# A quantile search over 32-bit masks: the bits and the count of a group in two sums over a constant in place of three sums

## The chip, the cores and the metric

The kernel runs on one NeuronCore of a Trainium2 chip. The metric is the device time of one execution in microseconds (us). Engines are named as in the profile: PE (matrix products) with PEld (its weight loads), DVE (vector), ACT (scalar, element by element), POOL and SP (here they mostly start DMA transfers). Sums of matrix products are made in PSUM, in banks of 512 float32 numbers per partition; ACT or DVE reads them out ("evicts" them).

## The reference

Four graph layers with a residual and a normalisation each, over 16 graphs of 1024 nodes with 64 channels. The change touches the third alone. There, every node takes, channel by channel, the 0.25, 0.5 and 0.75 quantiles of its neighbours' values (after some edges are dropped):

```python
vals = jnp.where(nd[..., None], x[:, None, :, :], jnp.inf)
s = jnp.sort(vals, axis=2)
nv = nd.sum(2)
agg = jnp.zeros_like(x)
for tau, w in zip(TAUS, WTS):
    pos = jnp.asarray(tau, x.dtype) * jnp.maximum(nv - 1, 0).astype(x.dtype)
    lo = jnp.floor(pos).astype(jnp.int32)
    hi = jnp.ceil(pos).astype(jnp.int32)
    ...
    agg = agg + jnp.asarray(w, x.dtype) * (v_lo + frac * (v_hi - v_lo))
```

`nd` is the neighbourhood matrix of a graph (1024 x 1024, zeros and ones), `lo` and `hi` are the places of the two values wanted among a node's sorted neighbours.

## The kernel before

Graphs go in pairs, eight pairs. For each pair the layers before the quantiles run first (attention takes most of their time), and beside the attention of one pair all 1024 node values of each channel of the pair ahead are sorted on DVE. Then the quantile stage of that pair runs (`quantiles`). This happens eight times.

*What the stage does.* For a channel, a node's neighbours are a set of ranks from 0 to 1023. The ranks are cut into 32 blocks (`T`) of 32 ranks (`R`). For each block and each node the kernel makes, by a matrix product with the neighbourhood matrix, a 32-bit mask (which ranks of this block are neighbours) together with a count (how many neighbours lie in earlier blocks). From the counts it finds the block in which the wanted neighbour lies, picks this block's mask, and searches the mask for the k-th set bit.

*Groups, pairs, units, steps.* Four channels make a group (`G` = 16 groups in a graph). A group with one of the three quantiles is a step; eight steps (`U8N`) make a unit. A stage has 96 steps, s = 0 to 7 in each of 12 units, and a group serves three steps, so a unit uses 8/3 groups.

*Elements and words.* `words_of` (L1086), at the end of the sort, splits a rank into block `rk` and place `r16` within the block, and makes from the place the powers of two that stand for its bit, by writing exponents of bfloat16 numbers as integers. `words` (L771) makes the weights `E` of a group on DVE, 128 x 1024 elements in one tile for each piece of the mask. The first is 16 for a rank in an earlier block, a power of two for the ranks 0 to 3 of the block itself, and 0 for later blocks (L786 and L787: a difference, clamped to 0 and 16). The second and third hold the ranks 4 to 17 and 18 to 31 (L789 and L791: a comparison, and a product with `b_w` for each). Up to seven such tiles (`EB`) are alive.

`half_word` (L854) sums one piece over all nodes, for half of the 1024 columns: eight matmuls with the neighbourhood matrix `ndT` into one bank, then one eviction (L862) that adds 8192 and writes uint16, so that, read as bfloat16, the piece is an ordinary number that a product with 0 or 1 leaves as it is. A group has three pieces, two halves each: six half sums of at most 14 bits.

*A step, s, on PE.* The order of PE's products in the loop is written out (`product`): `distances` for the step twelve back (`r,pen`, `kilo,pen`, `oh,bd`, four banks), the first part of the step's half sums, `least_values`, `one_hot` of the next step (`lt,dif`, four banks), `sum_values` (`vals,bonesf`), the rest of the half sums, and `sum_words` (`wps<-m,tonesb`). All banks come from one pool of four, in turn. `MORE` says how many half sums a step gets: (4, 3, 3, 3, 1, 1, 1, 0).

*A step on DVE.* `compare` (L867) finds by `lt` which blocks begin at or before the wanted place; `dif` on PE makes the difference of neighbouring blocks, ACT copies it as `oh` (one 1 per column); `pick` (L885) multiplies all three pieces by `oh`, once for each of the two places, into `m`; `sum_words` adds over the blocks. `lt` has one buffer, `m` has two, one for each of the two places.

*The bit search.* When a unit's eight steps are summed, ACT copies the sums (`wb`, L710) and `kth_bit` (L700) runs on DVE, in parts over the steps 0 to 4 of the next unit. It subtracts the 8192, takes the count from the first piece, and finds the k-th bit by counting bits in parts. Its last operations write `r64` and `r2` (L768, L769), which `distances` reads from step 4 on (`r,pen`). `more_elements` is called in the steps 4 to 7, but the order on DVE is set when the kernel is built, by priorities, and not by the place of the call.

Of the kernel before, what the change touches and what calls it, by code (L numbers as in the profile page):

```python
# [14 lines left out]
F16 = mybir.dt.float16  # L15
BF = mybir.dt.bfloat16
I32 = mybir.dt.int32
U16 = mybir.dt.uint16
# [12 lines left out]
T = 32  # L31
R = 32
NW = 3
OFF = 8192.0
G = C // 4
NQ = 3
U8N = 8
# [1 line left out]
GB = 4  # L39
PARTS = 4  # L40
LAG = PARTS + 1
MORE = (4, 3, 3, 3, 1, 1, 1, 0)
SC = 2048.0
VB = 4
EB = 7
# [15 lines left out]
def shape_constants():  # L61

    bf = ml_dtypes.bfloat16
    s = np.arange(N)
    t = np.arange(T)
    x = np.arange(8 * P)[None, :] - 3 * P
    tc = np.broadcast_to(t[:, None], (T, 2))

    p = np.arange(P)
    dif = np.eye(P) - ((p[:, None] == p[None, :] + 2) & (p[:, None] // C == p[None, :] // C))  # L70

    tones = np.zeros((P, U8N, 32))
# [12 lines left out]


    tof = np.zeros((2, 2, U8N, 4, NU, C))
    qrow = np.zeros((2, 2, U8N, 4, 3, 4))
    for u in range(NU):
        for i in range(U8N):  # L90
            g, q = divmod(U8N * u + i, NQ)
            for c in range(4):
                tof[:, :, i, c, u, 4 * g + c] = 1.0
            share = 0.25 * (q + 1)
            w = (0.25, 0.5, 0.25)[q] / SC
            for kk in range(2):
                qrow[:, kk, i, :, u % 3, :] = (share, kk - share - 0.375, -w, w)
    return {
        "c_t": np.broadcast_to(tc, (P, T, 2)).astype(np.uint16),
        "c_t16": np.broadcast_to(16.0 * tc, (P, T, 2)).astype(np.float16),  # L100
        "c_dif": dif.astype(bf),
        "c_bones": bones.astype(np.float32),
        "c_tones": tones.astype(bf),
        "c_tones4": tones[:, 0, :4].astype(np.float16),
        "c_pen": pen.reshape(P, U8N, 3, P).astype(np.float16),
        "c_tof": tof.reshape(P, NU, C).astype(np.float32),
        "c_qrow": qrow.reshape(P, 3, 4).astype(np.float32),
        "c_place": (np.sign(x - p[:, None]) + 1.0).astype(bf),
        "c_id": np.eye(P, dtype=np.float32),
        "c_idb": np.eye(P, dtype=np.float32).astype(bf),  # L110
        "c_idh": np.eye(P, dtype=np.float16),
        "c_iota": np.broadcast_to(s.astype(np.float16), (P, N)).copy(),
    }
# [3 lines left out]
def gnn_kernel(ctx: ExitStack, tc: tile.TileContext, a: dict, out: bass.AP):  # L117
# [22 lines left out]
    t16_c = load("t16_c", [P, T, 2], F16, a["c_t16"])  # L140
# [29 lines left out]
    tones4 = load("tones4", [P, 4], F16, a["c_tones4"])  # L170
    kilo = const.tile([P, 1], F16, name="kilo")
    nc.vector.memset(kilo, 1024.0)
    bn_a = const.tile([P, C], F32, name="bn_a")
    bn_b = const.tile([P, C], F32, name="bn_b")

# [42 lines left out]
    def bank(shape, dtype=F32):  # L218
        return ps1.tile(shape, dtype, name="bank")
# [439 lines left out]
    def rank_limits(gr, qe, qn):  # L659
# [14 lines left out]
        def limits(q):  # L674

            lim = gr.lim[q] = qe.tile([P, 2, N], U16, name="lim", bufs=LB)
            nc.scalar.activation(lim[:, 0], cnt, AF.Copy, scale=0.25 * (q + 1), bias=-0.25 * (q + 1) - 0.375)
            for s in (1, 0):
                nc.vector.tensor_scalar(lim[:, s], lim[:, 0], 16.0, OFF + 16.0 * (s + 1), op0=ALU.mult, op1=ALU.add)

        def weights(t):
            if t == 0:
# [17 lines left out]
    def kth_bit(pool, wps, kd, r2, r64):  # L700
# [9 lines left out]
        nc.scalar.copy(wb, wps)  # L710
        yield
        X = wb.bitcast(U16)
        v.tensor_scalar(X, X, OFF, None, op0=ALU.subtract)
        k = u16("k")
        S = u16("S", [P, 2, 512])
        U = u16("U", [P, 2, 512])
        a, c = U[:, 0], S[:, 0]
        v.tensor_scalar(a, X[:, 0], 4, None, op0=ALU.logical_shift_right)
        v.tensor_tensor(k, kd, a, ALU.subtract)
        v.tensor_scalar(X[:, 0], X[:, 0], 15, None, op0=ALU.bitwise_and)  # L720

        def counts(x, s1, s2, s4, t):

# [25 lines left out]
        v.tensor_scalar(pos, M[:, 0], 4.0, None, op0=ALU.mult)  # L749
# [21 lines left out]
    def words(pool, g, ws, rk, u_w, b_w):  # L771


        sh = [P, 2 * NB, T, 2]
        E = [pool.tile([P, NB, P], BF, name="E", bufs=EB) for w in ws]
        Ev = [e.rearrange("p j (h t c) -> p (j h) t c", h=2, t=T) for e in E]

        def over_t(x):
            return x[:, g].rearrange("p j (h c) -> p (j h) c", h=2)[:, :, None, :].to_broadcast(sh)

        def over_j(x):
            return x[:, None].to_broadcast(sh)

        if ws == [0]:
            d = Ev[0].bitcast(F16)
            nc.vector.tensor_tensor(d, over_j(t16_c), over_t(u_w), ALU.subtract)  # L786
            nc.vector.tensor_scalar(Ev[0], d, 0.0, 16.0, op0=ALU.max, op1=ALU.min)  # L787
        else:
            nc.vector.tensor_tensor(Ev[1], over_t(rk), over_j(t_c), ALU.is_equal)  # L789
            for w in range(2):  # L790
                nc.vector.tensor_tensor(Ev[w], Ev[1], over_t(b_w[w]), ALU.mult)  # L791
        return E

    def quantiles(ip, rk, u_w, b_w):
# [12 lines left out]
        with ExitStack() as es:  # L807
# [46 lines left out]
            def half_word(gr, g, w, hf, matmul):  # L854

                if (w, hf) == (0, 0):
                    gr.V[g] = qe.tile([P, NW, N], U16, name="V", bufs=VB)
                cols = slice(hf * 512, (hf + 1) * 512)
                ps = bank([P, 512])
                for j in range(NB):  # L860
                    matmul(ps, gr.E[g][w][:, j], gr.ndT[:, j, cols], start=(j == 0), stop=(j == NB - 1))
                nc.scalar.activation(gr.V[g][:, w, cols], ps, AF.Copy, bias=OFF)  # L862

            def compare(u, s):
                gr, g, q = u.pairs[s]
# [79 lines left out]
            halves = iter([(k, w, hf) for k in range(len(groups)) for w in range(NW) for hf in range(2)])  # L945
            todo = [(k, ws) for k in range(len(groups)) for ws in ([0], [1, 2])]
            made = used = 0

            def elements():

                nonlocal made
                k, ws = todo.pop(0)
                gr, g = groups[k]
                gr.E.setdefault(g, []).extend(words(qe, gr.bb * G + g, ws, rk, u_w, b_w))
                made += len(ws)

            def more_elements():
                while todo and made + len(todo[0][1]) <= used // 2 + EB:
                    elements()

            def more_words(n, matmul=product):
# [6 lines left out]

            load_matrix(graphs[0])
            with tc.high_priority():  # L970
                while made < 2 * NW:
                    elements()
            more_words(2 * NW, nc.tensor.matmul)
            more_elements()
            counts, limits, weights = rank_limits(graphs[0], qe, qn)
            for hf in range(2):
# [11 lines left out]
            for i, (u, s) in enumerate(steps):  # L988
# [97 lines left out]
    def words_of(pool, rank, rk, u_w, b_w):  # L1086
# [9 lines left out]
        m = pool.tile([P, 2 * G, NB, 4], U16, name="m16")  # L1096
        e = pool.tile([P, 2 * G, NB, 4], U16, name="e16")
        z = pool.tile([P, 2 * G, NB, 4], U16, name="z16")
        for w, first in ((2, 18), (1, 4), (0, 0)):
            dst = z if w == 0 else b_w[w - 1].bitcast(U16)  # L1100
            if w < 2:
                v.tensor_scalar(m, r16, float((4, 18)[w]), None, op0=ALU.is_lt)
            if w == 2:
                v.tensor_scalar(e, r16, 18.0, None, op0=ALU.is_ge)
            elif w == 1:
                v.tensor_scalar(e, r16, 4.0, None, op0=ALU.is_ge)
                v.tensor_tensor(e, e, m, ALU.mult)
            else:
                e = m
            v.tensor_scalar(dst, r16, float(127 - first), 128.0, op0=ALU.add, op1=ALU.mult)  # L1110
            v.tensor_tensor(dst, dst, e, ALU.mult)
        v.tensor_scalar(u_w, rk, 16.0, None, op0=ALU.mult)
        v.tensor_tensor(u_w, u_w, z.bitcast(BF), ALU.subtract)

    def sort(keys, pool, key, pace, rk, u_w, b_w):
# [52 lines left out]
        return key  # L1168

    rk = keep.tile([P, 2 * G, NB, 4], U16, name="rk")  # L1170
    u_w = keep.tile([P, 2 * G, NB, 4], F16, name="u_w")
    b_w = [keep.tile([P, 2 * G, NB, 4], BF, name=f"b_w{w}") for w in range(2)]

    def sort_keys(srt, ip):
        key = srt.tile([P, N], F32, name="key", bufs=2)
# [103 lines left out]
```

## Time and profile before

| | us |
|---|---|
| runs of before, median of 3 | 13250.63 (13241.73 to 13259.92) |
| the profiled execution | 13256.31 |
| its span | 13254.3 |
| PE busy in the span | 11579.9 (87%) |
| DVE busy | 10669.6 (80%) |
| ACT busy | 7184.3 (54%) |
| one quantile stage, 2835 to 3804 us: length | 969.0 |
| PE, DVE, ACT busy in it | 872.9, 831.7, 541.8 |

In a line of a group the profile shows the source line, the engine, the operation, what is written and read, the shape, how often it occurs, busy time and the mean duration of one (ns), and then how long the engine was idle just before and what ended that. In a timeline a row begins with the start and the busy time of a run of equal instructions; a wait ahead of it stands in brackets. Mean durations overlap: the next instruction starts before the last has ended, so the distance between starts is what one more costs.

### The profile page before, as it was taken

Reading aid. Unit: us, or ns where it says so; the run is one execution under the profiler, and the core shown is the slowest. Engines: PE = TensorE matmul, PEld = TensorE weight load, DVE = VectorE, ACT = ScalarE, POOL = GpSimd, SP = SyncE. Lnnn points to the kernel's source line nnn. Section 1 sums busy time; section 2 is a strip of 40 time slices with the busy share of each in tenths; the row PEclk is TensorE's granted clock in tenths of the full one; section 3 lists DMA queues with packets and bytes.
Section 4 is the critical chain, followed back from the end, with each engine's and each line's share of the span. In section 5 each row is a group of like instructions: output and inputs, shape, how many; then the busy total and the mean of one; then the engine's idle time right before and its main releaser. Section 6 shows DMA issues by size and latency. Waiting matters only on the chain.

```text
span 13254.3 us, 214818 instructions
## 1 busy us (share of the span) xinstructions
PE 11579.9 (87%) x85632; PEld 4955.8 (37%) x85632; DVE 10669.6 (80%) x18811; ACT 7184.3 (54%) x13164; POOL 552.7 (4%) x828
## 2 busy tenths in 40 slices
PE   7899897989979899798997989979898798983897
PEld 4555232543325433254333633336332363321232
DVE  3587997779977798777997789867898778978895
ACT  5655554556536555365653755536555465551553
POOL 0000000000000000000000000000000000000000
PEclk9999998999989999899998999989999899996998
DMA  2120003100031000310004100041000310002001
GB/s 78 54 79 20 5 5 102 61 19 5 5 114 51 17 5 6 125 41 15 5 5 134 33 14 5 6 135 34 11 6 23 119 38 7 8 23 77 4 5 45
DMA packets 352268, 510.43 MB, mean 39 GB/s; under 512 B 120481, under 2 KB 275489, under 8 KB 349217
## 3 DMA queue, kind: packets, MB, share of 16 engines
q1 hardware_dynamic: 288656, 367.77, 8.8%
q10 hardware_dynamic: 33040, 86.88, 2.0%
q0 software_dynamic: 29568, 42.05, 1.1%
q8 instruction: 673, 11.03, 0.4%
q14 instruction: 331, 2.70, 0.1%
HBM read 380.08 MB, written 116.46 MB: 37 GB/s over the span
## 4 chain that ended last, share of the span: by engine, by line
PE 45%; DVE 24%; issue 16%; ACT 8%; DMA 3%; POOL 0%; SPq 0%; ACTq 0%; DVEq 0%; POOLq 0%
PE bank L852 14%; PE banks L515 6%; PE bank L551 6%; PE bank L537 6%; DVE m L885 5%; ACT vals L918 4%; PE acc L852 3%; PE wps L852 3%; DMA at<-in_adjT 2%; PE bank L398 2%; DVE key L1124 1%; DVE lt L867 1%; PE banks L375 1%; PE bank L494 1%; DVE U L757 1%
## 5 line engine op out<-in xcount | busy, mean ns | idle before, releaser
L885 DVE TENSOR_TENSOR m<-V,oh 128x3072 bf16<-128x3072 bf16 x1536 | 2640.1, 1753 | 283.5 <-PE wps L852 262.8
L852 PE MATMUL bank<-ndT,E 128*128 128x512 fp8e4 x11904 | 2750.5, 380 | 106.5 <-ACT vals L918 98.8
L918 ACT ACTIVATE vals<-bank 128x512 f32<-128x512 f32 x3072 | 1586.9, 603 | 1525.7 <-PE bank L852 1524.9
L522 DVE CUSTOM_DVE_ANT_0 s<-banks,adj 128x1024 f32<-128x1024 f32 x1024 | 1214.6, 1222 | 801.9 <-PE banks L515 798.6
L852 PEld LDWEIGHTS <-E 128*128 128x128 bf16 x11904 | 1115.2, 98 | 1946.1 <-issue 780.0
L862 ACT ACTIVATE V<-bank 128x512 uint16<-128x512 f32 x1536 | 912.3, 597 | 1609.6 <-PE bank L852 1505.3
L876 ACT CAST oh<-bank 128x512 f16<-128x512 f32 x3072 | 1589.6, 623 | 125.4 <-PE bank L852 110.2
L541 ACT COPY pT<-bank 128x512 f32<-128x512 f32 x1536 | 801.5, 594 | 796.4 <-PE bank L537 796.2
L530 ACT ACTIVATE s<-s,mx 128x1024 f32<-128x1024 f32 x1024 | 1176.7, 1161 | 73.5 <-DVE mx L522 70.9
L852 PE MATMUL bank<-lt,dif 128*128 128x512 bf16 x3072 | 986.8, 387 | 235.7 <-DVE lt L867 79.9
L515 PE MATMUL banks<-kT,qT 64*128 64x512 f32 x4096 | 1092.1, 624 | 67.8 <-DVE mx L522 37.5
L867 DVE TENSOR_TENSOR lt<-V,lim 128x2048 bf16<-128x2048 uint16 x768 | 936.1, 1219 | 135.5 <-PE bank L852 132.2
L537 PEld LDWEIGHTS bank<-ident,s 128*128 128x128 f32 x8192 | 889.5, 141 | 401.6 <-issue 291.2
L537 PE MATMUL bank<-ident,s 128*128 128x128 f32 x8192 | 1021.1, 278 | 0.5 <-DVE pT L543 0.5
L551 PE MATMUL bank<-pT,v 128*64 128x256 f32 x8192 | 1000.4, 387 | 0.0
L852 PE MATMUL acc<-vals,bonesf 128*32 128x512 f32 x6144 | 973.3, 611 | 0.3 <-ACT vals L918 0.3
L852 PE MATMUL bank<-oh,bd 64*64 64x512 f16 x12288 | 848.2, 395 | 0.0
L852 PE MATMUL wps<-m,tonesb 128*32 128x512 bf16 x9216 | 645.0, 382 | 150.0 <-DVE m L885 149.3
L852 PE MATMUL bank<-r,pen 32*128 32x512 f16 x6144 | 491.0, 386 | 264.3 <-DVE r L769 240.6
L551 PEld LDWEIGHTS bank<-pT,v 128*64 128x64 f32 x8192 | 546.3, 137 | 309.8 <-issue 45.0
L515 PEld LDWEIGHTS banks<-kT,qT 64*128 64x128 f32 x4096 | 395.8, 190 | 537.5 <-issue 336.1
L1124 DVE TENSOR_TENSOR key<-key 128x512 f32<-128x512 f32 x880 | 582.1, 690 | 0.8
(252 smaller groups left out, 12820.5 us busy)
## 6 DMA issues: line engine op xcount, KB each, us to landing
at<-in_adjT SPq DMA_DIRECT2D x256, 512.0 KB, 5.2
masks_d<-mask SPq DMA_DIRECT2D x440, 128.0 KB, 1.7
mask<-masks_d SPq DMA_DIRECT2D x440, 128.0 KB, 2.1
adj<-in_adj SPq DMA_DIRECT2D x96, 512.0 KB, 5.2
ad<-in_adj ACTq DMA_DIRECT2D x64, 512.0 KB, 4.4
agg_d<-vals POOLq DMA_DIRECT2D x96, 256.0 KB, 2.3
agg<-agg_d ACTq DMA_DIRECT2D x16, 1536.0 KB, 7.2
nd_d<-nd SPq DMA_DIRECT2D x128, 128.0 KB, 2.0
```

Source lines behind the costliest of these rows:

```text
L515: then(nc.tensor.matmul(ss[h][:, hf * 512:(hf + 1) * 512], gr.qk[hp, 0][HALF[h], k * P:(k + 1) * P], gr.qk[hp, 1][HALF[h], hf * 512:(hf + ...
L522: last = nc.vector.tensor_tensor_reduce(s, ss[h], gr.adj[k], -1.0, 3.0e38, ALU.add, ALU.min, mx)
L530: then_act(nc.scalar.activation(s, s, AF.Exp, bias=mx, scale=-1.0, accum_out=sm))
L537: then(nc.tensor.transpose(ps[:, m, :], exps[h][0][:, (4 * mh + m) * P:(4 * mh + m + 1) * P], ident))
L541: then_act(nc.scalar.copy(dst, ps))
L551: then(nc.tensor.matmul(po[HALF[h]], gr.v[:, 4 * mh + m, (2 * hp + h) * C:(2 * hp + h + 1) * C], pT[h][mh][:, m, :], start=(mh == 0 and m ...
L852: then(nc.tensor.matmul(*args, **kw))
L862: nc.scalar.activation(gr.V[g][:, w, cols], ps, AF.Copy, bias=OFF)
L867: nc.vector.tensor_tensor(u.lt, gr.V[g][:, None, 0, :].to_broadcast([P, 2, N]), gr.lim[q], ALU.is_lt)
L876: nc.scalar.copy(oh[:, kk, cols], ps)
L885: picked = nc.vector.tensor_tensor(u.m[kk], gr.V[g].bitcast(BF), u.oh[s][:, kk, None, :].to_broadcast([P, NW, N]), ALU.mult)
L918: nc.scalar.activation(vals[t], ys[t], AF.Relu)
```

## The change

The 32 bits and the count go into two sums in place of three. The first has the count in units of 2048, the ranks 0 to 4 at bits 6 to 10 and the ranks 13 to 18 at bits 0 to 5. The second has the ranks 5 to 12 at bits 0 to 7 and the ranks 19 to 31 at bits 8 to 20. Each sum starts with one more matmul that puts a constant into the bank, 2^21 or 2^23 (32 rows of 2^16 or 2^18, times one). With it the float32 number in PSUM has a fixed exponent, and its lowest byte holds the lowest 6 (times 4) or 8 bits of the sum. Two evictions follow: one scales the upper part down to uint16, the other reads the lowest byte of each number and writes it into every second byte of the third piece, the high bytes from the first sum and the low bytes from the second.

`V` keeps three pieces: the count with 5 bits, 14 bits, 13 bits. So `lt`, `m`, `wps` and `wb` keep their shapes. The elements of a group are two tiles in place of three. `MORE` becomes (1, 3, 3, 3, 1, 0, 0, 0), with one less in step 3 of every third unit; ahead of the loop four and three half sums are made in place of six and four. `words_of` writes other exponents, from three comparisons, and `u_w` is now uint16.

```diff
-MORE = (4, 3, 3, 3, 1, 1, 1, 0)
+MORE = (1, 3, 3, 3, 1, 0, 0, 0)
+EW = 2
+OFF0 = 128.0
+MAGIC = (2.0 ** 21, 2.0 ** 23)
...
+    magic = const.tile([32, EW, P], BF, name="magic")
+    for w in range(EW):
+        nc.vector.memset(magic[:, w], MAGIC[w] / 32)
+    ones5 = const.tile([32, 512], BF, name="ones5")
+    nc.vector.memset(ones5, 1.0)
...
-                nc.vector.tensor_scalar(lim[:, s], lim[:, 0], 16.0, OFF + 16.0 * (s + 1), op0=ALU.mult, op1=ALU.add)
+                nc.vector.tensor_scalar(lim[:, s], lim[:, 0], 32.0, OFF0 + 32.0 * (s + 1), op0=ALU.mult, op1=ALU.add)
...
-        v.tensor_scalar(X, X, OFF, None, op0=ALU.subtract)
+        v.tensor_scalar(X[:, 0], X[:, 0], OFF0, None, op0=ALU.subtract)
+        v.tensor_scalar(X[:, 1:3], X[:, 1:3], OFF, None, op0=ALU.subtract)
...
-        v.tensor_scalar(a, X[:, 0], 4, None, op0=ALU.logical_shift_right)
+        v.tensor_scalar(a, X[:, 0], 5, None, op0=ALU.logical_shift_right)
...
-        if ws == [0]:
-            d = Ev[0].bitcast(F16)
-            nc.vector.tensor_tensor(d, over_j(t16_c), over_t(u_w), ALU.subtract)
-            nc.vector.tensor_scalar(Ev[0], d, 0.0, 16.0, op0=ALU.max, op1=ALU.min)
+        if w == 0:
+            d = Ev.bitcast(F16)
+            nc.vector.tensor_tensor(d, over_j(tk_c), over_t(u_w), ALU.subtract)
+            nc.vector.tensor_scalar(Ev, d, 0.0, 2048.0, op0=ALU.max, op1=ALU.min)
         else:
-            nc.vector.tensor_tensor(Ev[1], over_t(rk), over_j(t_c), ALU.is_equal)
-            for w in range(2):
-                nc.vector.tensor_tensor(Ev[w], Ev[1], over_t(b_w[w]), ALU.mult)
+            nc.vector.tensor_tensor(Ev, over_t(rk), over_j(t_c), ALU.is_equal)
+            nc.vector.tensor_tensor(Ev, Ev, over_t(b_w), ALU.mult)
...
                 ps = bank([P, 512])
+                matmul(ps, magic[:, w], ones5, start=True, stop=False)
                 for j in range(NB):
-                    matmul(ps, gr.E[g][w][:, j], gr.ndT[:, j, cols], start=(j == 0), stop=(j == NB - 1))
-                nc.scalar.activation(gr.V[g][:, w, cols], ps, AF.Copy, bias=OFF)
+                    matmul(ps, gr.E[g][w][:, j], gr.ndT[:, j, cols], start=False, stop=(j == NB - 1))
+                low = ps.bitcast(U8).rearrange("p (n b) -> p n b", b=4)[:, :, 0]
+                both = gr.V[g][:, 1, cols].bitcast(U8).rearrange("p (n b) -> p n b", b=2)
+                if w == 0:
+                    nc.scalar.activation(gr.V[g][:, 0, cols], ps, AF.Copy, scale=2.0 ** -6,
+                                         bias=OFF0 - MAGIC[0] / 64 - 63 / 128)
+                    nc.scalar.activation(both[:, :, 1], low, AF.Copy, scale=0.25, bias=OFF / 256)
+                else:
+                    nc.scalar.activation(gr.V[g][:, 2, cols], ps, AF.Copy, scale=2.0 ** -8,
+                                         bias=OFF - MAGIC[1] / 256 - 255 / 512)
+                    nc.scalar.copy(both[:, :, 0], low)
...
             with tc.high_priority():
-                while made < 2 * NW:
+                while made < 2 * EW:
                     elements()
-            more_words(2 * NW, nc.tensor.matmul)
+            more_words(2 * EW, nc.tensor.matmul)
...
-            more_words(4)
+            more_words(3)
...
-                more = MORE[s]
+                more = MORE[s] - (s == 3 and u.n % 3 == 2)
...
-        for w, first in ((2, 18), (1, 4), (0, 0)):
-            dst = z if w == 0 else b_w[w - 1].bitcast(U16)
...
-            v.tensor_scalar(dst, r16, float(127 - first), 128.0, op0=ALU.add, op1=ALU.mult)
-            v.tensor_tensor(dst, dst, e, ALU.mult)
+        for e, least in zip(ge, (5.0, 13.0, 19.0)):
+            v.tensor_scalar(e, r16, least, None, op0=ALU.is_ge)
...
+        v.tensor_scalar(z, ge19, -6.0, 122.0, op0=ALU.mult, op1=ALU.add)
+        v.tensor_tensor(z, z, r16, ALU.add)
+        v.tensor_tensor(z, z, ge5, ALU.mult)
+        v.tensor_scalar(dst, z, 128.0, None, op0=ALU.mult)
...
+        v.tensor_scalar(u_w, rk, 2048.0, 1024.0, op0=ALU.mult, op1=ALU.add)
         v.tensor_tensor(u_w, u_w, z.bitcast(BF), ALU.subtract)
```

More of the change, by code (lines that the diff above doesn't have):

```diff
@@ L99, in shape_constants @@
         "c_t": np.broadcast_to(tc, (P, T, 2)).astype(np.uint16),
-        "c_t16": np.broadcast_to(16.0 * tc, (P, T, 2)).astype(np.float16),
+        "c_tk": np.broadcast_to(2048 * tc + 1024, (P, T, 2)).astype(np.uint16),
         "c_dif": dif.astype(bf),
@@ L139, in gnn_kernel @@
     t_c = load("t_c", [P, T, 2], U16, a["c_t"])
-    t16_c = load("t16_c", [P, T, 2], F16, a["c_t16"])
+    tk_c = load("tk_c", [P, T, 2], U16, a["c_tk"])
     dif = load("dif", [P, P], BF, a["c_dif"])
@@ L717, in kth_bit @@
         a, c = U[:, 0], S[:, 0]
-        v.tensor_scalar(a, X[:, 0], 4, None, op0=ALU.logical_shift_right)
+        v.tensor_scalar(a, X[:, 0], 5, None, op0=ALU.logical_shift_right)
         v.tensor_tensor(k, kd, a, ALU.subtract)
-        v.tensor_scalar(X[:, 0], X[:, 0], 15, None, op0=ALU.bitwise_and)
+        v.tensor_scalar(X[:, 0], X[:, 0], 31, None, op0=ALU.bitwise_and)
         def counts(x, s1, s2, s4, t):
@@ L748, in kth_bit @@
         pos = u16("pos")
-        v.tensor_scalar(pos, M[:, 0], 4.0, None, op0=ALU.mult)
+        v.tensor_scalar(pos, M[:, 0], 5.0, None, op0=ALU.mult)
         v.tensor_scalar(a, M[:, 1], 14.0, None, op0=ALU.mult)
@@ L769, in kth_bit, with words @@
         v.tensor_tensor(r2, pos, pos, ALU.mult)
-    def words(pool, g, ws, rk, u_w, b_w):
+    def words(pool, g, w, rk, u_w, b_w):
         sh = [P, 2 * NB, T, 2]
-        E = [pool.tile([P, NB, P], BF, name="E", bufs=EB) for w in ws]
-        Ev = [e.rearrange("p j (h t c) -> p (j h) t c", h=2, t=T) for e in E]
+        E = pool.tile([P, NB, P], BF, name="E", bufs=EB)
+        Ev = E.rearrange("p j (h t c) -> p (j h) t c", h=2, t=T)
         def over_t(x):
@@ L943, in quantiles @@
             steps = [(u, s) for u in units for s in range(U8N)]
-            halves = iter([(k, w, hf) for k in range(len(groups)) for w in range(NW) for hf in range(2)])
-            todo = [(k, ws) for k in range(len(groups)) for ws in ([0], [1, 2])]
+            halves = iter([(k, w, hf) for k in range(len(groups)) for w in range(EW) for hf in range(2)])
+            todo = [(k, w) for k in range(len(groups)) for w in range(EW)]
             made = used = 0
@@ L951, in elements @@
                 nonlocal made
-                k, ws = todo.pop(0)
+                k, w = todo.pop(0)
                 gr, g = groups[k]
-                gr.E.setdefault(g, []).extend(words(qe, gr.bb * G + g, ws, rk, u_w, b_w))
-                made += len(ws)
+                gr.E.setdefault(g, []).append(words(qe, gr.bb * G + g, w, rk, u_w, b_w))
+                made += 1
             def more_elements():
-                while todo and made + len(todo[0][1]) <= used // 2 + EB:
+                while todo and made + 1 <= used // 2 + EB:
                     elements()
@@ L1094, in words_of @@
         v.tensor_scalar(r16, r16, 31, None, op0=ALU.bitwise_and)
-        m = pool.tile([P, 2 * G, NB, 4], U16, name="m16")
-        e = pool.tile([P, 2 * G, NB, 4], U16, name="e16")
+        ge = [pool.tile([P, 2 * G, NB, 4], U16, name=f"ge{i}") for i in range(3)]
         z = pool.tile([P, 2 * G, NB, 4], U16, name="z16")
-        for w, first in ((2, 18), (1, 4), (0, 0)):
-            dst = z if w == 0 else b_w[w - 1].bitcast(U16)
[L1101 to L1109, printed above, removed]
-            v.tensor_scalar(dst, r16, float(127 - first), 128.0, op0=ALU.add, op1=ALU.mult)
-            v.tensor_tensor(dst, dst, e, ALU.mult)
-        v.tensor_scalar(u_w, rk, 16.0, None, op0=ALU.mult)
+        for e, least in zip(ge, (5.0, 13.0, 19.0)):
+            v.tensor_scalar(e, r16, least, None, op0=ALU.is_ge)
+        ge5, ge13, ge19 = ge
+        v.tensor_tensor(ge5, ge5, ge13, ALU.subtract)
+        v.tensor_tensor(ge5, ge5, ge19, ALU.add)
+        dst = b_w.bitcast(U16)
+        v.tensor_scalar(z, ge19, -6.0, 122.0, op0=ALU.mult, op1=ALU.add)
+        v.tensor_tensor(z, z, r16, ALU.add)
+        v.tensor_tensor(z, z, ge5, ALU.mult)
+        v.tensor_scalar(dst, z, 128.0, None, op0=ALU.mult)
+        v.tensor_scalar(z, ge13, -19.0, 133.0, op0=ALU.mult, op1=ALU.add)
+        v.tensor_tensor(z, z, r16, ALU.add)
+        v.tensor_scalar(ge5, ge5, -128.0, 128.0, op0=ALU.mult, op1=ALU.add)
+        v.tensor_tensor(z, z, ge5, ALU.mult)
+        v.tensor_scalar(u_w, rk, 2048.0, 1024.0, op0=ALU.mult, op1=ALU.add)
         v.tensor_tensor(u_w, u_w, z.bitcast(BF), ALU.subtract)
@@ L1170, in gnn_kernel @@
     rk = keep.tile([P, 2 * G, NB, 4], U16, name="rk")
-    u_w = keep.tile([P, 2 * G, NB, 4], F16, name="u_w")
-    b_w = [keep.tile([P, 2 * G, NB, 4], BF, name=f"b_w{w}") for w in range(2)]
+    u_w = keep.tile([P, 2 * G, NB, 4], U16, name="u_w")
+    b_w = keep.tile([P, 2 * G, NB, 4], BF, name="b_w")
     def sort_keys(srt, ip):
```

## The prediction, made before the changed kernel was run

> **What bounds the kernel now.** I read the windows of the quantile stage first (each row: window, its length, then busy time and count of PE, PEld, DVE, ACT, POOL, then granted clock and DMA). The stage runs eight times, once for a pair of graphs, each time for some 970 us (1205 to 2183 us the first time). Two full units of the eight-step loop and the last ones:
>
> ```profile
> 1728.70:1803.30 74.60, 69.33 (x576) 23.32 (x575) 68.07 (x100) 43.22 (x82) 0.56 (x1) 1.00 0.01 5
> 1803.30:1877.70 74.40, 69.84 (x581) 23.57 (x578) 68.28 (x102) 43.73 (x82) 4.87 (x9) 1.00 0.02 6
> ...
> 2025.50:2096.20 70.70, 59.56 (x524) 18.67 (x520) 60.71 (x86) 39.48 (x75) 0.58 (x2) 0.96 0.01 5
> ```
>
> PE is busy 94% and DVE 92% of a unit: neither alone is the bound, ACT (59%) is not. Next, PE's timeline in one unit shows who decides when:
>
> ```profile
> 1741.33 0.61 PE L852 MATMUL bank<-r,pen 32*128 32x512 f16 x8
> ...
> 1748.84 0.61 PE L852 MATMUL bank<-r,pen 32*128 32x512 f16 x8
> ...
> 1754.40 0.61 PE L852 MATMUL bank<-r,pen 32*128 32x512 f16 x8
> ...
> 1766.71 0.61 PE L852 MATMUL bank<-r,pen 32*128 32x512 f16 x8
> ...
> 1777.29 0.61 PE L852 MATMUL bank<-r,pen 32*128 32x512 f16 x8
> ...
> 1787.86 0.61 PE L852 MATMUL bank<-r,pen 32*128 32x512 f16 x8
> ...
> 1800.41 0.83 PE L852 MATMUL wps<-m,tonesb 128*32 128x512 bf16 x12 [1.91 <-DVE m L885]
> 1801.18 0.61 PE L852 MATMUL bank<-r,pen 32*128 32x512 f16 x8
> ```
>
> Every step on PE begins with `r,pen`, so the starts give the step lengths: step 6 (one half sum) 7.5 us, step 7 (none) 5.56, step 0 (four) 12.3, steps 1 and 2 (three) 10.6, step 3 (three) 13.3, of which 2.6 are waits for DVE. A half sum costs 1.82 to 1.89 us. While PE runs steps 0 to 3, DVE works through the bit search without a pause; in steps 4 to 7 DVE waits for PE. Last, the groups:
>
> ```profile
> L885 DVE TENSOR_TENSOR m<-V,oh 128x3072 bf16<-128x3072 bf16 x1536 | 2640.1, 1753 | 283.5 <-PE wps L852 262.8
> L852 PE MATMUL bank<-ndT,E 128*128 128x512 fp8e4 x11904 | 2750.5, 380 | 106.5 <-ACT vals L918 98.8
> L862 ACT ACTIVATE V<-bank 128x512 uint16<-128x512 f32 x1536 | 912.3, 597 | 1609.6 <-PE bank L852 1505.3
> L791 DVE TENSOR_TENSOR E<-E,b_w 128x1024 bf16<-128x1024 bf16 x512 | 350.9, 685 | 75.3 <-PE bank L852 51.8 <-PE bank L861 22.1
> ```
>
> The words' matmuls are PE's largest group, and DVE waits for PE (`wps`) more than for anything else.
>
> **The change, part by part.**
>
> *PE, words.* 1536 half sums of 8 matmuls become 1024 of 9 (8 and the constant): 12288 to 9216. One matmul is 2750.5/11904 = 0.231 us of PE's time, in a full unit 0.227 (59.0 us for 256 in 1803 to 1952 us). A half sum becomes 9 x 0.227 = 2.04 us, a unit has 10.67 in place of 16: 16 x 1.82 - 10.67 x 2.04 = 7.4 us less work for PE, 650 us over some 88 units. It is not all time, since DVE follows at once. The constant's matmul has 32 rows; the trace has none like it alone. Bounds: 0.055 us (the eight `r,pen` matmuls, also of 32 rows, in 0.44 us side by side) and 0.386 (the mean of one of those); I take the 0.227 of its neighbours, since nothing stands beside it.
>
> *ACT, words.* A half sum is evicted twice. Per unit 21.3 evictions in place of 16: 5.3 x 0.6 = 3.2 us on an engine that is 59% busy. But the bank is held longer, and banks rotate by four: `pen` of the next step begins with the bank of the step's last half sum. Now that is just in time (an eviction ends at 1733.83, `pen` starts at 1733.88), so the second eviction is a wait for PE in steps 0 to 4. Reading single bytes and writing every second byte is not in the trace. The 512-element evictions take 597, 603 and 623 ns whatever type they write, and four in a row take 2.06 us, so one more adds 0.49. Bounds: 0 (hidden), and 0.7, from `kc` at L688 with 0.81, the slowest 512-element form. No gain is possible from an added eviction. I take 0.48.
>
> *DVE, elements.* One product with `b_w` less per group: 256 x 0.685 = 175 us of busy time, at the 0.61 between starts 1.6 us a unit. The first difference now takes two uint16 operands; L789 with uint16 operands takes the same 0.685, so nothing.
>
> *DVE, the rest.* L713 in two pieces: 0.46 + 0.29 busy for 0.55, but the shift that follows needs only the first piece, so between starts nothing changes (0.59 before; 0.2 + 0.34 after). `words_of`: eight scalar operations as before, products from 5 to 7, 1.2 us a pair, 40 us ahead of the stage (at 1164 us) under the attention's PE work; without that cover, in the last pair, 2 us once. Three memsets at the start: under the loads. The limits' constants change nothing.
>
> *DVE, order.* The changed kernel's instruction order leaves all stages but this one alone. In a unit the bit search and the elements move later: before, `r` (L769), which opens step 4 on PE, stood ahead of step 3's `m` in seven of the eleven units that have it, and at most one short operation behind it in two more; now it stands 1 to 3.6 us behind it in eight, and in the last unit behind step 4's `m`.
>
> *The sum.* Two rules follow from the dependencies. DVE ends step i's `m` pair at the later of (its last pair's end + its work between) and (PE's last `wps` + 3.43, the pair itself: it reuses the buffer). PE ends step i's `wps` at the later of (its last `wps` + its own step length) and (`m`'s end + 0.87). A step on PE is 5.56 us without words ahead of the one-hots, 5.14 with (10.6 - 3 x 1.82), plus its half sums. DVE's work per step comes from the instruction order and the distances between starts in the timeline (`m` pair 3.34, `lt` 1.14, elements 0.61 / 0.34 / 0.61, the search 24 in all).
>
> Checked on before, the unit after 1754.40, DVE's steps 0 to 7 being 4.5, 15.4, 13.6, 12.7, 6.7, 5.1, 4.5, 5.7: `wps` ends at 12.3, 22.9, 33.5, 46.3 (there DVE decides: `m` at 45.4), 53.7, 61.2, 68.6, 74.2. The trace: 12.3, 22.9, 33.5, 46.8, and units of 74.2 to 74.8.
>
> After, DVE's steps: 4.5, 10.8, 13.6, 14.6, 8.4, 5.1, 4.5, 4.5; PE's: 5.56 + 2.04 + 0.48 = 8.1; 5.14 + 3 x 2.04 + 0.48 = 11.75, twice; 9.7 (two half sums; 11.75 in the other units); 8.1; 5.56, three times. `m` ends at 3.4, 14.2, 27.8, 42.4; `wps` at 8.1, 19.8, 31.6, 43.3 (DVE decides). `r` follows `m` of step 3 by 2.7 + 0.1: 45.2, so PE waits 1.9 us at the start of step 4 and ends it at 53.3; then 58.9, 64.4, 70.0. So 70.0 for 74.2: of the 7.4 us that PE loses, 4.2 are time; what is late next is DVE's search.
>
> The same over the stage's other units, each with its own order: units 2 to 9 together -30.1 us, units 0, 1 and 10 together -10.1, and the last unit +4.6 (`r` comes 11 us late in place of 2.3, which the trace shows at 2093.65). That is -35.6. At the stage's head ten half sums (13.3 + 7.1 us) become seven (10.1 + 6.0): -4. Eight stages: 8 x 39.6 = -317. The profiled execution took 13256.3 us (span 13254.3), 5.7 above the median of the runs: 13256.3 - 317 - 5.7 = **12,933 us**.
>
> Bounds: eviction at 0, -43 a stage in place of -35.6, 12,876; at 0.7, 12,963; the constant's matmul at 0.386, 12,985, at 0.055, 12,898; both dear ends, 13,035.
>
> **Rivals.**
>
> *The search does not delay PE* (`r` in time, as in most units of before): -49 + -4 a stage, 12,826. For: DVE could gain on PE in steps 4 to 7. Against: PE's last `wps` holds every `m`.
>
> *PE's clock falls*, since PE waits more. The stretch from 2025 to 2096 us has PE 84% busy and a clock of 0.96, full units 1.00 at 92 to 94%; after, PE has 62.3 busy in 70.3 us, 89%. At 0.96 steps 4 to 7 and part of 0 to 3 stretch, some 1.5 us a unit: 88 x 1.5 = 132, 13,065. Against: the unit of 1577 to 1652 us with 91.6% still has 1.00. [...]
>
> *DVE alone decides and keeps its idle time.* DVE's work falls by about 1.5 us a unit (68.3 to 66 to 67.5), and its 6 us of idle remain, if the waits only move: 88 x 1.5 + 32 = 164, 13,087. For: DVE is 92% busy. Against: its idle time now is waits for `wps` in steps 4 to 7, and those steps get shorter.
>
> *Slower: the byte evictions are dear.* Place: the bank of a step's last half sum. PE's steps add up to 67.5 us with 0.48; five of them hold words, so 67.5 - 2.4 + 5e reaches 74.2 at e = 1.8, from where ACT decides. At four times the 0.597 of L862 (2.4, one for each byte of a word) e is 2.3: 76.6 a unit, 88 x 2.4 - 32 = +179, 13,430. For: no row shows such an access. Against: three output types cost the same. [...]
>
> *It does not do what it says*: if the bits are not exact, work and time are the same, as no step depends on the data. If the saving is eaten wholly, no change.
>
> **How the numbers follow.** Forecast with its bounds (12,876 to 13,035) 0.52; search in time, 0.13; clock, 0.10; DVE with its idle time, 0.13; dear bytes, 0.09; nothing measurable, 0.03. The range 12,800 to 13,095 holds the forecast, the first three rivals' values with little room around them, about 0.8. Faster by over 0.2% (27 us, what a measurement of this kernel can tell): 0.88; same 0.03; slower 0.09.
>
> **What would show it.** Units of some 70 us in the windows of the stage; PE's words 9216 in number and about 2130 us; `r,pen` waiting 1 to 2.4 us for DVE `r` at step 4, and about 11 us in a stage's last unit; `pen` waiting near 0.5 us for ACT `V` after a half sum; the byte copies at 0.6 us; clock 1.00 in full units. It is wrong if byte evictions take over 1 us, if units stay at 73 us or more, or if PE's step 4 begins without a wait.

## The result, and the profile after

| | before | after |
|---|---|---|
| median of 4 runs, us | 13247.51 (13241.73 to 13259.92) | 13022.99 (13016.84 to 13032.38) |
| span of the profiled execution | 13254.3 | 13020.6 |
| first stage, from ACT's copy `t_pr` at its head to its last store to `agg_d` | 969.4 | 942.2 |
| PE, DVE, ACT busy | 11579.9, 10669.6, 7184.3 | 11213.3, 10504.1, 7349.8 |

The changed kernel takes 0.983 of the time before, 95% interval 0.9813 to 0.9847: 224.5 us less, where 317 were forecast. In the first stage the gain is 27.2 us, in the next six 27.2 to 28.2, so some 220 us of it are in the eight quantile stages.

The engines' shares of the chain of waits in the changed kernel (before, PE had 45% of that chain, DVE 24%, ACT 8%):

```profile
PE 49%; issue 16%; DVE 14%; ACT 12%; DMA 3%; POOL 0%; ACTq 0%; SPq 0%; DVEq 0%; POOLq 0%
```

DVE lost share of this chain, PE and ACT gained. The groups of the changed kernel, different shapes apart:

```profile
L903 DVE TENSOR_TENSOR m<-V,oh 128x3072 bf16<-128x3072 bf16 x1536 | 2636.1, 1753 | 274.8 <-PE wps L860 227.5 <-issue 39.0 <-ACT V L880 2.0
L860 PE MATMUL bank<-ndT,E 128*128 128x512 fp8e4 x7936 | 1913.4, 385 | 0.0
...
L860 PE MATMUL bank<-r,pen 32*128 32x512 f16 x6144 | 611.4, 390 | 394.4 <-DVE r L778 344.2 <-ACT V L876 16.6 <-ACT cnt L680 5.6
L860 PE MATMUL bank<-ones,magic 32*128 32x512 bf16 x992 | 383.5, 387 | 86.8 <-ACT vals L936 72.4 <-ACT oh L894 9.1
...
L876 ACT ACTIVATE V<-bank 128x512 uint8<-128x512 uint8 x512 | 304.5, 595 | 0.0
L880 ACT COPY V<-bank 128x512 uint8<-128x512 uint8 x512 | 298.7, 583 | 0.0
L799 DVE TENSOR_TENSOR E<-E,b_w 128x1024 bf16<-128x1024 bf16 x256 | 174.9, 683 | 0.8
```

A byte eviction takes 595 or 583 ns, no more than the 597 of the float ones. The words' matmuls in the loop went from 2750.5 us to 1913.4 + 383.5 = 2296.9. With those ahead of the loop (98.5 before; 72.7 and 15.1 after) all 9216 have 2384.7 us of busy time; the prediction said about 2130. `r,pen` now waits 344 us for DVE's `r` (240.6 before): 13 us more a stage, of which the last unit has 8.6 in the first stage (10.93 us for 2.29).

Two full units in the windows of the changed kernel (columns as in the prediction), and PE's timeline of the second, `r,pen` alone, so that each step's start is seen:

```profile
1663.66:1733.93 70.27, 66.52 (x551) 20.76 (x547) 66.80 (x101) 45.38 (x88) 4.94 (x9) 1.00 0.03 6
1733.93:1804.11 70.18, 66.68 (x551) 20.91 (x547) 66.15 (x99) 45.36 (x87) 4.86 (x9) 1.00 0.02 6
```

```profile
1733.78 0.61 PE L860 MATMUL bank<-r,pen 32*128 32x512 f16 x8
1741.61 1.06 PE L860 MATMUL bank<-r,pen 32*128 32x512 f16 x8
...
1753.93 1.07 PE L860 MATMUL bank<-r,pen 32*128 32x512 f16 x8
...
1766.26 1.07 PE L860 MATMUL bank<-r,pen 32*128 32x512 f16 x8
...
1778.61 1.06 PE L860 MATMUL bank<-r,pen 32*128 32x512 f16 x8
...
1786.88 1.07 PE L860 MATMUL bank<-r,pen 32*128 32x512 f16 x8
1792.84 0.61 PE L860 MATMUL bank<-r,pen 32*128 32x512 f16 x8
```

These two take 70.3 and 70.2 us; the full unit that the prediction worked through was to take 70.0. The steps 1, 2 and 3 take 12.33 each (forecast 11.75), step 4 8.27, and at step 4 there is no wait for `r` in this unit and 0.48 in the unit before it. After a step with half sums the eight `r,pen` take 1.06 instead of 0.61, since some of them wait for the bank of the last half sum (the run with every byte eviction made twice shows it below: five of the eight wait 0.70 us for `V`).

So the loss against the forecast is hardly in the full units. Lengths of the first stage's parts, from the start of one `wb` copy on ACT to the next (unit 0 with the head; the last unit with the stage's tail). On record is the forecast by groups alone: -30.1 for units 2 to 9, -10.1 for 0, 1 and 10, -4 for the head (here in 0), +4.6 for the last. The last row splits them by unit, by the prediction's two rules; this split was worked out afterwards:

| unit | 0 | 1 | 2 | 3 | 4 | 5 | 6 | 7 | 8 | 9 | 10 | last |
|---|---|---|---|---|---|---|---|---|---|---|---|---|
| before | 83.9 | 78.9 | 74.1 | 78.2 | 74.8 | 77.1 | 74.2 | 74.8 | 74.1 | 74.3 | 74.2 | 130.9 |
| after | 81.5 | 76.7 | 70.1 | 75.0 | 75.4 | 74.7 | 70.3 | 70.2 | 71.2 | 70.3 | 70.2 | 136.8 |
| change | -2.4 | -2.2 | -4.0 | -3.2 | +0.6 | -2.4 | -3.9 | -4.6 | -2.9 | -4.0 | -4.0 | +5.9 |
| forecast | -5.7 | -2.8 | -3.7 | -2.2 | -5.2 | -3.6 | -3.2 | -5.3 | -3.7 | -3.2 | -5.6 | +4.6 |

The forecast's sum is -39.6, the measured one -27.1. The largest part of the miss is unit 4: 5.8 of 12.5 us. Its step 0 on PE, then ACT's rows in the same stretch, then a window of it, all of the changed kernel:

```profile
1515.60 0.86 PE L860 MATMUL bank<-lt,dif 128*128 128x512 bf16 x2
1519.63 1.06 PE L860 MATMUL bank<-lt,dif 128*128 128x512 bf16 x2 [3.16 <-ACT vals L936]
1520.62 1.94 PE L860 MATMUL acc<-vals,bonesf 128*32 128x512 f32 x8
1522.49 0.60 PE L860 MATMUL bank<-ones,magic 32*128 32x512 bf16 x1
1523.03 2.83 PE L860 MATMUL bank<-ndT,E 128*128 128x512 fp8e4 x8
```

```profile
1514.96 1.08 ACT L936 ACTIVATE vals<-bank 128x512 f32<-128x512 f32 x2
1518.28 0.81 ACT L696 ACTIVATE kc<-cnt,qrow 64x512 uint16<-64x512 f16 x1 [2.24 <-DVE k L728]
1519.00 1.05 ACT L936 ACTIVATE vals<-bank 128x512 f32<-128x512 f32 x2
```

```profile
1519.60:1523.00 3.40, 3.37 (x11) 0.40 (x10) 3.26 (x7) 3.17 (x6) 0.00 (x0) 0.50 0.00 0
```

Read them from ACT. Between two pairs of `vals` evictions stands `kc` (L696), a weight for the second graph's search; its buffer is free only when DVE's search of the unit before has read it (`k`, L728), 2.24 us later. Behind it wait the evictions, for these PE's `lt,dif` (their bank), 3.16 us. Then PE runs at half clock (0.50 in the window): `vals,bonesf` takes 1.94 where it takes 1.07 elsewhere, the eight words 2.83 for 1.90; from the start of `vals,bonesf` to the next `r,pen` it is 5.93 against 3.91 elsewhere. 3.16 + 2.0 are nearly all of the 5.3 us by which step 0 is longer here (13.09 against 7.83). Before, `kc` waited as long, 2.30 us, as ACT's first row shows, but two half sums stood ahead of `lt,dif` on PE, as PE's rows show (kernel before, timeline):

```profile
1533.18 0.81 ACT L688 ACTIVATE kc<-cnt,qrow 64x512 uint16<-64x512 f16 x1 [2.30 <-DVE k L719]
```

```profile
1530.44 3.61 PE L852 MATMUL bank<-ndT,E 128*128 128x512 fp8e4 x16 [0.33 <-ACT vals L918]
1534.53 0.86 PE L852 MATMUL bank<-lt,dif 128*128 128x512 bf16 x2
1536.46 0.86 PE L852 MATMUL bank<-lt,dif 128*128 128x512 bf16 x2 [1.08 <-ACT V L862]
```

`MORE` went from 4 to 1 in step 0, and 1 // 2 = 0 half sums stand there now. Before, this step 0 took 14.28 us, against 12.31 in unit 7. Unit 5's step 0 has the same 3.16 us wait in the changed kernel (12.45 us).

### The profile page after: what moved, and what is told of

Read it like the earlier page. It is cut to its first block, busy times and chain, and to the rows that moved or that the text cites. A ratio compares the mean times of both kernels' runs of the same rounds, so it can differ in the third digit from the quotient of the medians.

```text
span 13020.6 us, 208990 instructions
## 1 busy us (share of the span) xinstructions
PE 11213.3 (86%) x82479; PEld 4663.4 (36%) x82560; DVE 10504.1 (81%) x18670; ACT 7349.8 (56%) x13676; POOL 554.7 (4%) x828
## 4 chain that ended last, share of the span: by engine, by line
PE 49%; issue 16%; DVE 14%; ACT 12%; DMA 3%; POOL 0%; ACTq 0%; SPq 0%; DVEq 0%; POOLq 0%
PE bank L860 18%; PE banks L523 6%; PE bank L559 6%; PE bank L545 6%; ACT vals L936 6%; PE acc L860 4%; DVE m L903 3%; DMA at<-in_adjT 2%; PE wps L860 2%; DVE key L1142 1%; PE bank L406 1%; PE banks L383 1%; ACT V L876 1%; ACT V L878 1%; ACT V L880 1%
## 5 line engine op out<-in xcount | busy, mean ns | idle before, releaser
L860 PE MATMUL bank<-ndT,E 128*128 128x512 fp8e4 x7936 | 1913.4, 385 | 0.0
L860 PE MATMUL bank<-lt,dif 128*128 128x512 bf16 x3072 | 1072.3, 393 | 322.8 <-DVE lt L885 75.5
L860 PEld LDWEIGHTS <-E 128*128 128x128 bf16 x7936 | 700.0, 98 | 1055.9 <-issue 366.7
L860 PE MATMUL bank<-r,pen 32*128 32x512 f16 x6144 | 611.4, 390 | 394.4 <-DVE r L778 344.2
L860 PE MATMUL wps<-m,tonesb 128*32 128x512 bf16 x9216 | 656.5, 387 | 70.1 <-DVE m L903 70.1
L874 ACT ACTIVATE V<-bank 128x512 uint16<-128x512 f32 x512 | 305.6, 597 | 656.5 <-PE bank L860 602.0
L878 ACT ACTIVATE V<-bank 128x512 uint16<-128x512 f32 x512 | 305.9, 598 | 639.6 <-PE bank L860 629.3
```

The source lines that it names most:

```text
L860: then(nc.tensor.matmul(*args, **kw))
L878: nc.scalar.activation(gr.V[g][:, 2, cols], ps, AF.Copy, scale=2.0 ** -8, bias=OFF - MAGIC[1] / 256 - 255 / 512)
```

## The experiments

*The theory*: the missing 100 us (8 x 12.5; by the medians it is 92.5) lie in units where small ACT work for the second graph stalls PE, and which lost their cover. *The rivals*: the byte evictions or the constant's matmul cost more than forecast in all units; or DVE alone sets the length, so that PE's savings are worth less everywhere.

**Two more `kc` buffers.** The wait for `k` goes; nothing else in the program's text changes:

```diff
-            kc = gr.kc[t] = qn.tile([P, 512], U16, name="kc", bufs=4)
+            kc = gr.kc[t] = qn.tile([P, 512], U16, name="kc", bufs=6)
```

> The changed kernel with six buffers for kc in place of four, nothing else. Theory A (the second graph's weights make ACT wait for the bit search, in the middle of the evictions of step 0; that step's half sums, which used to cover it, are gone): the waits of 3.16 us ahead of lt,dif in two units of a stage go, these units fall from 75.4 and 74.7 us to about 70.5, so 9 us a stage, 70 us in all: 12,950. Rival B (the wait is only where DVE's lateness shows; DVE decides the unit): within 15 us of the changed kernel, 13,010 to 13,025.

Measured: 13019.68 (13013.94 to 13026.53), ratio 0.9825 (0.9809 to 0.9842): nothing. A miss of the total, and of the mechanism in one of two units. As expected, the wait of L696 falls from 37.9 us to 1.7, and unit 4 from 75.4 to 70.1, just as a full unit. But unit 3 grows from 75.0 to 79.1: without the wait the builder places the weights earlier, among unit 3's own work, where they stall the same matmuls. And unit 5 stays at 74.7: its step 0 falls from 12.45 to 7.83, and its steps 3 and 4 grow by as much, since PE now waits there for DVE's `r` and for an eviction (this kernel, PE's timeline):

```profile
1501.43 2.06 PE L860 MATMUL bank<-lt,dif 128*128 128x512 bf16 x4 [2.46 <-ACT vals L936]
1503.41 1.94 PE L860 MATMUL acc<-vals,bonesf 128*32 128x512 f32 x8
...
1640.66 0.39 PE L860 MATMUL bank<-r,pen 32*128 32x512 f16 x3 [1.84 <-DVE r L778]
1643.85 1.01 PE L860 MATMUL bank<-r,pen 32*128 32x512 f16 x5 [2.80 <-ACT V L876]
```

**The same in the kernel before**, as a control: if unit 4 paid for `kc` before as well, it gains there too.

> The kernel before, with six buffers for kc. Theory A: there two half sums stand between the distances and the one-hots of step 0 and cover the wait, so at most 15 us: 13,230 to 13,250. Rival B': the wait cost as much before, so -70 us, 13,180.

Measured: 13300.13 (one run), some 50 us slower than the kernel before beside it (13249.74) and outside both forecasts: unit 3 goes from 78.2 to 82.3, unit 5 from 77.1 to 78.3. Unit 4 stays at 74.8: its step 0 falls from 14.28 to 12.30, and its step 3 grows from 11.35 to 13.32, where PE waits longer for DVE's `m` (1.92 us for 0.71). So before, the wait in unit 4 cost step 0 some 2 us, and step 3 took them up; its unit felt nothing. After, it costs the unit 5.3 us: the change uncovered it.

**Every byte eviction twice.**

```diff
-                    nc.scalar.activation(both[:, :, 1], low, AF.Copy, scale=0.25, bias=OFF / 256)
+                    for _ in range(2):
+                        nc.scalar.activation(both[:, :, 1], low, AF.Copy, scale=0.25, bias=OFF / 256)
...
-                    nc.scalar.copy(both[:, :, 0], low)
+                    for _ in range(2):
+                        nc.scalar.copy(both[:, :, 0], low)
```

> The changed kernel, each byte eviction made twice (the same values). Theory A (PE decides the full units, and the bank that is held for the second eviction is a wait for PE): 0.49 us more at pen in five steps and at the one-hots in three, up to 3.9 us a unit, 13,250 to 13,360. Rival B (DVE's search decides, PE has slack): under 13,080.

Measured: 13261.87 (one run), +239, as theory A expected. Full units take 74.5 (every third 72.3) for 70.2. Two waits in one step grew (this kernel, PE's timeline):

```profile
1758.19 0.59 PE L860 MATMUL bank<-r,pen 32*128 32x512 f16 x5 [0.70 <-ACT V L882]
...
1764.10 0.38 PE L860 MATMUL bank<-lt,dif 128*128 128x512 bf16 x1 [0.57 <-ACT oh L896]
```

One more byte eviction thus costs some 0.9 us in each of the five steps with half sums (4.3 / 5), at two places. The first one, by the changed kernel's `r,pen` (1.06 for 0.61), costs 0.45 at the place where the forecast charged 0.48. The rival that the bytes themselves are dear falls: it needs 1.8.

**Without the constant's matmul.** The first of the eight starts the bank, and the offsets are taken out of the evictions' biases.

```diff
-                matmul(ps, magic[:, w], ones5, start=True, stop=False)
...
-                    matmul(ps, gr.E[g][w][:, j], gr.ndT[:, j, cols], start=False, stop=(j == NB - 1))
+                    matmul(ps, gr.E[g][w][:, j], gr.ndT[:, j, cols], start=(j == 0), stop=(j == NB - 1))
```

> The changed kernel without the constant's matmul (and without its offset in the evictions): the split of a sum into its bytes is left out in effect, so the third piece and the picked values are not the reference's; all other work stays. Theory A: a half sum falls from 2.15 to 1.83, 3.4 us less for PE in a unit, until the search decides: units of 67 to 69 us, 12,800 to 12,930. Rival B (DVE decides now): units stay at 70, 12,990 to 13,025.

Measured: 12932.86 (one run), -90, between the two forecasts and close to A's. But the full units 2 and 6 to 9 stay at 69.7 to 71.6: the steps 1 and 2 fall from 12.33 to 11.28, and what PE gains it loses at step 4, where it waits 2.3 to 4.1 us for `r` (unit 7 of this kernel, PE's timeline, then a window behind the wait):

```profile
1768.30 1.04 PE L860 MATMUL bank<-r,pen 32*128 32x512 f16 x8 [2.29 <-DVE r L778]
...
1769.70 1.92 PE L860 MATMUL bank<-oh,bd 64*64 64x512 f16 x16
```

```profile
1768.30:1771.00 2.70, 2.70 (x28) 0.84 (x28) 2.67 (x4) 0.12 (x1) 0.00 (x0) 0.50 0.01 3
```

In four of the six full units of the changed kernel PE decides, but DVE's `r` is close behind it: where PE is quicker, as here, it takes over, and the clock is 0.50 in the window behind the wait. The 90 us come from other units, above all 3 (71.2 for 75.0), 4 (70.5 for 75.4) and 10, a full unit in which `r` is in time (66.5 for 70.2).

**The larger part of a step's half sums ahead of the one-hots**, so that step 0's only one covers `kc` again:

```diff
-                more_words(more // 2)
+                more_words(more - more // 2)
...
-                more_words(more - more // 2)
+                more_words(more // 2)
```

> The changed kernel with the larger part of a step's half sums ahead of the one-hots and the smaller behind (one half sum stands ahead, three are two and one). Theory A: the half sum ahead of the one-hots in step 0 covers most of ACT's wait for kc (2 of 3.2 us, twice a stage), and in steps 0 and 4 no bank is held into pen and the one-hots find banks free: 0.3 and 0.6 us a unit less. Together 4 + 11 x 0.9 = 14 us a stage: 12,910. Rival B (DVE decides): 13,000 to 13,040.

Measured: 12929.87 (12923.35 to 12940.21), ratio 0.9763 (0.9747 to 0.9779). Unit 4 falls to 73.4, unit 3 to 73.4, the full units 6 to 10 to between 68.6 and 70.5; unit 2 grows to 71.7. Units 6 to 10 together give 5.7 us a stage, unit 4 gives 2.0: most of the gain is not the cover for `kc`. The 3.16 us wait has become two shorter ones (this kernel, PE's timeline):

```profile
1518.11 0.86 PE L860 MATMUL bank<-lt,dif 128*128 128x512 bf16 x2 [1.17 <-ACT vals L936]
1520.51 0.58 PE L860 MATMUL bank<-lt,dif 128*128 128x512 bf16 x1 [1.54 <-ACT V L880]
1521.03 1.94 PE L860 MATMUL acc<-vals,bonesf 128*32 128x512 f32 x8
```

**Both**, six buffers and this order:

> The changed kernel with both, six buffers for kc and the larger part ahead. Theory A: the rest of the kc wait goes too, 12,870 to 12,900. If the two act on the same wait alone, no better than the better of the two by themselves.

Measured: 12928.59 (one run), no better than the order alone. A miss of theory A: unit 4 falls to 69.3, but unit 3 rises to 77.9. The buffers move the stall and don't remove it.

**The search ahead of step 4's `m`** in a stage's second and last unit, where `r` is 18 and 11 us late: the `m` pair of step 4 (`picked`) gets a dependence in DVE's order on the search's last operation.

```diff
+        found.append(v.tensor_tensor(r2, pos, pos, ALU.mult))
...
+                    if s == PARTS and u in (units[1], units[-1]):
+                        tc.add_manual_dep(picked.ins, found[-1].ins.name, in_order, reason="after the search")
```

> The changed kernel, where in the second and the last unit of a stage the m pair of step 4 waits behind the search's last operation (an order on DVE, no work changed). Theory A (in the last unit PE stands 10.9 us for r, since m of step 4 and its lt stand ahead of it): r comes some 3.5 us earlier in both, 7 us a stage, 56 in all: 12,967. Rival: what PE gains at step 4 it loses at that step's end, where m is later: 13,015 to 13,025.

Measured: 12984.26 (12969.61 to 12986.82), ratio 0.98 (0.9785 to 0.9815), -39. Unit 1 takes 73.6 for 76.7; the last unit, up to its own `wb` copy, 66.8 for 70.1. The wait for `r` falls from 18.29 to 15.19 in unit 1 and from 10.93 to 7.84 in the last: 3.1 us of each were this order on DVE, and what the rest is was not tested. The total missed the 12,967 expected by 17 us.

**All three edits:**

> The three together: six buffers for kc, the larger part ahead, and the search ahead of m of step 4 in the second and last unit. Theory A: the savings add, since each takes away another wait: 12,820 to 12,860. If they share a wait, 12,890.

Measured: 12888.31 (12879.97 to 12900.14), ratio 0.973 (0.9716 to 0.9745): not the 12,820 to 12,860 of theory A. The order ahead of the one-hots and the search add up (-93 and -39); the buffers add nothing. So, last, **without the buffers**:

> The changed kernel with the larger part of a step's half sums ahead of the one-hots, and with the search ahead of step 4's `m` pair in a stage's second and last unit; `kc` keeps its four buffers. Theory A, the two extra `kc` buffers were worth nothing, since the weights' waits only moved into unit 3: the two edits add up, -93 and -39, so 12,880 to 12,900 us. Rival B, the buffers did carry part of the best run's gain (they let the second graph's weights go early, where the half sum ahead of the one-hots can cover them): 12,910 to 12,930. Unit 4 tells them apart as well: 73 us by A, and unit 3 back at 73 to 74.

Measured: 12883.26 (12875.20 to 12894.80), ratio 0.9723 (0.971 to 0.9736); unit 3 at 73.4, unit 4 at 71.8. Theory A held. This version, two small edits of order on the changed kernel, beats both kernels: 140 us under the changed one.

## Why the prediction was right, and where it was not

*Direction, range and the largest term hold.* 13,022.99 lies in 12,800 to 13,095. Full units were to take 70.0, and the six of them (2, 6 to 10) take 70.1 to 71.2. One product with `b_w` less took 176 us off DVE, as costed; uint16 operands cost nothing (L795, 683 ns; 685 before with float16); the byte evictions cost what float ones do (595 and 583 ns, 597 before); the last unit's wait for `r`, forecast at 11, is 10.93 (timeline at 2062.19).

*The half sum and the step on PE were sized low.* 2.04 us was forecast; the starts of the constants show 2.15 (1748.87 to 1751.02): 0.32 for the constant, 1.83 for its eight neighbours. The constant was priced at a neighbour's 0.227. (That figure is 1.82 us in eight parts; the 59.0 us for 256 that the prediction gives for it make 0.230.) A second cost was not in the sum: where a half sum stands ahead of the one-hots, the fourth `dif` waits for its bank, and the group takes 1.22 us between starts for 0.97. Together 3 x 0.11 + 0.25 = 0.58, which is 12.33 less 11.75.

*So full units are right for the forecast's reason in two of six.* The prediction worked through a unit with two half sums in step 3. Units 2 and 8 are of this kind: step 4 begins 45.2 us behind step 0 in both, as forecast, with `r` 1.83 and 1.84 us late (1.9 forecast), so there DVE's search decides. Unit 8 takes 71.2 us for unit 2's 70.1, since PE runs at half clock behind this wait (0.50 in 1850.50 to 1852.50; step 4 takes 8.90 for 7.82). In units 6, 7, 9 and 10, with three half sums in step 3, PE decides step 3 itself, and `r` is 0 to 0.5 us late. The prediction had named a step 4 that begins without a wait as a sign of being wrong. Here the two errors cancel in the unit's length, since a PE as quick as forecast would have waited for `r`: in the run without the constant `r` is 2.29 us late in unit 7, and the unit is hardly shorter (69.7). It is no floor of the kernel: with the larger part ahead full units take 68.6.

*The step that failed* is the sum over "the stage's other units, each with its own order". It followed PE and DVE in each unit, and ACT in none. ACT was taken as an engine with room (59% busy), which it is; but it takes its work in order, as its rows above show, and in unit 4 the weights of the second graph stand in it waiting for DVE. By the split above the forecast gave this unit -5.2; it got +0.6. Two things hid the wait before: step 0's two half sums ahead of the one-hots, the very work that the change takes away, and the wait for DVE's `m` in step 3. The prediction costed the half sums' removal as a gain and did not name them as cover. That the wait costs unit 4 its 5.3 us now and cost it nothing before is shown: taking it away gives them back (six buffers), and gives nothing there in the kernel before (the control). One half sum put back as cover is weaker evidence: it gives 2.0, but the same edit gives up to 1.6 in full units. And the same wait in unit 5 costs nothing, since a later wait takes its place when it goes. So the stall is worth 8 x 5.3 = 42 us of the missing 100, not all of them as the theory had it.

*The rest of the miss.* Head and unit 0 gave 3.3 less than forecast: the head's first words take 11.3 us (1210.68 to 1221.98; forecast 10.1, before 13.2), the first 7 us of them at a clock of 0.50 (0.59 before), so that what goes is not in proportion; and in unit 0 the steps with three half sums take 8.9 us where they took 7.4, with 0.5 us waits for the bank. Unit 10 gave 1.6 less, the last unit 1.3, unit 5 1.2. These were not taken apart by a run, and their cause stays open. Unit 5's `r,pen` waits 2.08 us for an eviction behind the limits on ACT (L685, itself 2.71 us late by DVE's `lt`), but it waited 2.16 us there before too, so this is no part of the miss.

*The rivals.* "The search does not delay PE" fell: 8 x 13 us more of waits for `r`. "DVE alone decides" fell: full units shortened by 4, not by 1.5. "The clock falls" was right in kind, in other places: five of the six full units hold 1.00, but unit 8 falls to 0.98, unit 4 to 0.95 (1.00 before), where it pays 2.0 us, and the last unit up to its own `wb` copy to 0.88 (0.95 before). The forecast's sum has no term for the clock behind PE's waits: that waits of 1 to 2.4 us leave it alone no run shows, and the changed kernel had both, 1.00 behind 1.83 us in unit 2 and 0.50 behind 1.84 in unit 8.

## What to carry to other kernels

Before removing filler work, ask which other engine's in-order queue it was covering: here an engine that is 56% busy holds PE for 3.16 us when a small operation in the middle of its queue waits. Whether such a wait costs time depends on what waits behind it: the same 3.16 us cost one unit all of it and the next unit nothing. Where two engines stand as close together as here, only part of the work saved on one was time (4.0 us in a full unit, of 7.4 by the prediction's estimate), and the next saving was worth little while the other stayed (without the constant, unit 7 took 69.7 us for 70.2). More buffers did not remove the stall by themselves: they let the order change, and in this kernel that cost as much as it gave (13019.68 us for 13022.99).

## What the hardware showed unexpectedly

Behind waits of PE of 1.83 to 3.16 us, and behind two shorter ones close together, the clock was halved in some places and full in others. The granted clock was 0.50 behind 3.16 us in unit 4 (1519.60 to 1523.00), 2.29 in the run without the constant (1768.30 to 1771.00), and 1.84 in unit 8 (1850.50 to 1852.50), but 1.00 behind 2.08 in unit 5 (1639.00 to 1642.00) and 1.83 in unit 2 (1413.50 to 1416.50). Two kernels with the same pair of waits in unit 4, 1.17 and then 1.54 or 1.55 us, differ: the run with the larger part ahead has the slow rows shown above, at a clock of 0.53 (1520.50 to 1524.00); the last run has these, at 1.00 (1514.00 to 1520.00; its PE timeline):

```profile
1514.41 0.86 PE L862 MATMUL bank<-lt,dif 128*128 128x512 bf16 x2 [1.17 <-ACT vals L940]
1516.82 0.38 PE L862 MATMUL bank<-lt,dif 128*128 128x512 bf16 x1 [1.55 <-ACT V L882]
1517.12 1.06 PE L862 MATMUL acc<-vals,bonesf 128*32 128x512 f32 x8
```

So in these runs the length of a wait alone does not decide. What decides was not shown: no run here varied only the time at which a wait falls.

ACT's reads of every fourth byte out of PSUM took no longer than its reads of whole floats: 595 and 583 ns, against 597.
